# A new order of a software-pipelined period, with VectorE block transposes and three accumulating banks in the aggregation

## The chip, the cores and the metric

The kernel runs on one core of one Trainium2 chip. The metric is device time in microseconds for one execution. Five engines work side by side, each through its own queue in order: TensorE (PE; its weight loads are listed as PEld), VectorE (DVE), ScalarE (ACT), GpSimd (POOL) and SyncE (SP), which here only issues DMA transfers.

## The reference

There are 64 independent batches of 256 nodes with 512 features, all in 32-bit floats, and one 256x256 adjacency matrix. Two layers are applied to each batch, each as a residual step after a normalization and a ReLU:

```python
h = relu(layernorm(x))
x = x + gat(h, adj, W, a_src, a_dst)             # layer 0
h = relu(layernorm(x))
x = x + mha(h, adj, Wq, bq, Wk, bk, Wv, bv, Wo, bo)   # layer 1, 8 heads of 64

# gat:  Wh = h @ W; logits = leaky_relu(e_src[:, None] + e_dst[None, :], 0.2)
#       out = softmax(logits where adj else -inf) @ Wh
# mha:  q, k, v = h @ W.T + b; softmax(q k / 8 where adj) @ v; out @ Wo.T + bo
```

## The kernel before

**Tiling.** A batch is two row tiles of 128 nodes. Layer 0 first aggregates and then projects: `aggregate0` computes (attention weights) times h into `uT`, feature-major, and `transform0` multiplies `uT` by W and adds the rows to x. Layer 1 normalizes (`normalize1` writes `xn`), transposes to the feature-major `hT` (`transpose1`), projects (`project_qk`, `project_v`), attends (`attention`), divides by the row sums (`scale`) and projects back (`output`).

**Seven products.** Each big product of 2x2 blocks is computed with seven block products in place of eight. GpSimd forms four sums of the left blocks (`combine`: hs from hT, us from uT, as from aT, hq from h); the weight side is summed once. `chained` runs the seven in the order 0, 2, 1, 4, 3, 6, 5 and accumulates them in three PSUM banks called a, b and d: products 0, 1, 3, 5 go into bank a, product 2 into b, products 4 and 6 into d. A bank is read after each product, so the next product on the same bank must wait for that read. `assemble` does the reads: ScalarE copies after products 0, 1, 4, 5, VectorE adds after 2, 3, 6. In `transform0` and `output` VectorE makes all seven reads, each an add into x (line 768 before). The aggregation of layer 0 doesn't use `chained`: it uses `products`, with seven banks of its own and no accumulation, and `add_up`, which makes seven VectorE adds.

**The period.** One loop over i runs pieces of many batches at once. Each stage is a generator, and a list names which generator goes one step forward, and for which batch relative to i. The lists are written out by hand and nothing reorders them, so they fix the order in every engine's queue. The letters: K is `project_qk`, V `project_v`, W `transform0`, O `output` (seven products each); A is `attention` (a step for the scores and exponentials, four for masks and sums of two heads each, one for the values, the row sums and the transfers of the reciprocals); AS is `scale` (one step that multiplies, one that forms the sums); U0 and US are `aggregate0`; X1 is `transpose1`, N0 and N1 the normalizations, D0 the step that computes the two scores of the nodes and broadcasts one of them by DMA, E0 the edge weights, Q0 the quarters' sums, BO a bias.

```python
K, V, W, O = (project_qk, 0), (project_v, 0), (transform0, 1), (output, -2)
first_half = [
    (load, 3), O, D0, K, AS_OLD, O, K, O, K, O, K, E0, O, US, BO, A_OLD, K, E0, O, K, O, K,
]
second_half = [
    A_OLD, A, Q0, Q0, A, W, N0, W, W, V, N0, W, W, W, N1, W, N1, A, V, V, V, A, N0, N1, V, U0, AS,
    U0, X1, V, X1, V, X1,
]
```

**What crosses engines.** `attention` ends with the row sums `psm` on TensorE, reciprocals `rc` on VectorE, and twelve DMA issues of SyncE that broadcast them: four into `rb0` (for layer 0 of a later batch) and eight into `rb` (four for the first half of the heads, then four for the second). `scale` multiplies `aT[0]` and `aT[1]` by the halves of `rb` on VectorE; `output` needs `aT` so scaled, and from its third product on the GpSimd sums `as`. The tiles `hT`, `xn`, `uT`, `rb`, `rc`, `aT` and others have one buffer each (`h` has two, x six); the eight PSUM banks go round in the order in which they are asked for. A tile with one buffer is written for the next batch only when the last reader of the batch before has ended. For `hT` that reader is the last product of V.

Of the kernel before, what the change touches and what calls it, by code (L numbers as in the profile page):

```python
# [23 lines left out]
Q = 32  # L24
# [4 lines left out]
def kernel(  # L29
# [102 lines left out]
    def bounded():  # L132
# [34 lines left out]
            nc.gpsimd.tensor_tensor(s[:, 2], a(0, 0), a(1, 0), op=ALU.subtract)  # L167
            nc.gpsimd.tensor_tensor(s[:, 3], a(0, 1), s[:, 1], op=ALU.subtract)

        def products(a, s, name, product, read, order=range(7)):  # L170


            plan = (
                (a(0, 0), B11),
                (s[:, 1], T2),
                (a(0, 1), B21),
                (s[:, 2], T3),
                (s[:, 0], T1),
                (a(1, 1), T4N),
                (s[:, 3], B22),  # L180
            )
            for n in order:
                left, slot = plan[n]
                ps = bank([P, D], f"{name}_{n}")
                product(ps, left, slot)
                read(n, ps)
                yield

        CHAIN = ((0, "a"), (2, "b"), (1, "a"), (4, "d"), (3, "a"), (6, "d"), (5, "a"))

        def chained(a, s, name, product, read):
# [20 lines left out]
        def assemble(n, ps, dst, copy):  # L212
# [12 lines left out]
                nc.vector.tensor_add(dst(0, 1), dst(0, 1), ps)  # L225
            elif n == 5:
                copy(dst(1, 0), ps, 0)

        def add_up(n, ps, dst, s2):

            if n == 1:
                nc.vector.tensor_add(s2, dst(0, 0), ps)
            elif n == 2:
                nc.vector.tensor_add(dst(0, 0), dst(0, 0), ps)
            elif n == 3:
                nc.vector.tensor_add(dst(1, 0), s2, ps)
            elif n == 4:
                nc.vector.tensor_add(dst(1, 1), dst(1, 0), ps)
                nc.vector.tensor_add(dst(0, 1), s2, ps)
            elif n == 5:  # L240
                nc.vector.tensor_add(dst(1, 0), dst(1, 0), ps)
            elif n == 6:
                nc.vector.tensor_add(dst(0, 1), dst(0, 1), ps)

        def product_rows(wt, dst, left, slot, first):
            for c in range(2):
# [292 lines left out]
        def normalize0(g):  # L539

            xt = xts[g]
            h = big.tile([P, NT, D], F32, tag="h", name=f"h_{g}", bufs=2)
            es = small.tile([P, NT], F32, tag="es", name=f"es_{g}")
            ed = small.tile([P, NT], F32, tag="ed", name=f"ed_{g}")
            if g == 1:

                mv, rstd = norm_stats(xt, f"0_{g}", small)
                nmr = small.tile([P, NT], F32, tag="nmr", name=f"nmr0_{g}")
                nc.gpsimd.tensor_scalar(nmr, mv[:, :, 0], -1.0, 0.0, op0=ALU.mult, op1=ALU.add)
                nc.gpsimd.tensor_tensor(nmr, nmr, rstd, op=ALU.mult)  # L550
                yield
            else:
                stats = Stats(xt, h, f"0_{g}")
                for t in range(NT):
                    stats.mean(t)
                yield
                for t in range(NT):
                    stats.squares(t)
                nmr, rstd = stats.close()
                yield  # L560
            for t in range(NT):
                nc.scalar.activation(  # L562
                    h[:, t, :], xt[:, t, :], AF.Relu, bias=nmr[:, t : t + 1], scale=rstd[:, t : t + 1]
                )
            yield
            for t in range(NT):
                for dst, a in ((es, 0), (ed, 1)):
                    junk = work.tile([P, D], F32, tag="e2", name=f"junk_{g}_{t}")
                    nc.vector.scalar_tensor_tensor(  # L569
                        junk, (wa if g else pas)[a], 1.0, h[:, t, :], op0=ALU.mult, op1=ALU.mult,  # L570
                        accum_out=dst[:, t : t + 1],
                    )
            nodes[g] = h, es, ed
            if g >= PLAIN:

                row = work.tile([1, TOK], F32, tag="rc", name=f"es_row_{g}")
                for t in range(NT):
                    nc.sync.dma_start(row[:, t * P : (t + 1) * P], es[:, t : t + 1])
                es_b = work.tile([P, TOK], F32, tag="esum", name=f"es_b_{g}")
                spread(es_b, row)  # L580
                nodes[g] = h, es_b, ed
            yield
# [83 lines left out]
        def aggregate0(g):  # L666

            h, parts = nodes.pop(g)[0:2]
            em = edges[g][0]
            uT = big.tile([P, DC, TOK], F32, tag="uT", name=f"uT_{g}")  # L670
            if g >= PLAIN:
                left, s, right = parts
                s2 = work.tile([P, 4, P], F32, tag="s2", name=f"s2u_{g}")

                def product(dst, left, slot):
                    for e in range(2):
                        nc.tensor.matmul(
                            dst[:, e * P : (e + 1) * P], left[:, e * P : (e + 1) * P], right[slot],
                            start=True, stop=True,
                        )  # L680

                def dst(i, j):
                    return uT[:, 2 * i : 2 * i + 2, j * P : (j + 1) * P]

                def read(n, ps):
                    ps = ps[:, 0:HD].rearrange("p (e n) -> p e n", e=2)
                    if n == 0:
                        nc.scalar.copy(dst(0, 0), ps)
                    add_up(n, ps, dst, s2[:, 0:2, :])

                step_of = products(left, s, f"pu_{g}", product, read)
                for n in range(7):
                    next(step_of)
                    if n in (3, 6):
                        yield
                assert next(step_of, END) is END
            for dp in range(0, DC, 2) if g < PLAIN else ():
                pu = bank([P, 2, N], f"pu_{g}_{dp}")
                for d in range(2):
                    for m in range(NC):  # L700
                        nc.tensor.matmul(
                            pu[:, d, :],
                            h[:, m, (dp + d) * P : (dp + d + 1) * P],
                            em[:, m, :],
                            start=(m == 0),
                            stop=(m == NC - 1),
                        )
                nc.vector.tensor_mul(
                    uT[:, dp : dp + 2, :], pu, edges[g][1].unsqueeze(1).to_broadcast([P, 2, N])
                )  # L710
                yield

            def a(t, j):
                return uT[:, 2 * j : 2 * j + 2, t * P : (t + 1) * P]

            del edges[g]
            sums0[g] = a, four_sums("us", g)
            combine(a, sums0[g][1])
            yield
# [57 lines left out]
        def normalize1(g):  # L777
# [16 lines left out]
                xn = big.tile([P, NT, D], F32, tag="xn", name=f"xn_{g}")  # L794
            for t in range(NT):
                nc.scalar.activation(
                    xn[:, t, :], xt[:, t, :], AF.Identity,
                    bias=nmr[:, t : t + 1], scale=rstd[:, t : t + 1],
                )
            norms[g] = xn  # L800
# [4 lines left out]
        def transpose1(g):  # L805
# [5 lines left out]
            def a(t, j):  # L811
                return hT[:, 2 * j : 2 * j + 2, t * P : (t + 1) * P]

            for t in range(NT):
                pt = bank([P, DC, P], f"pt_{g}_{t}")
                for c in range(DC):
                    nc.tensor.transpose(pt[:, c, :], xn[:, t, c * P : (c + 1) * P], ident)
                nc.scalar.activation(hT[:, :, t * P : (t + 1) * P], pt, AF.Relu)  # L818
                yield
            lefts[g] = a, four_sums("hs", g)  # L820
            combine(a, lefts[g][1])
# [264 lines left out]
        def aside(n=1):  # L1086
            for _ in range(n):
                next(side, END)

        K, V, W, O = (project_qk, 0), (project_v, 0), (transform0, 1), (output, -2)  # L1090
        N0, D0, E0, U0 = (normalize0, 3), (normalize0, 2), (weights0, 2), (aggregate0, 2)
        Q0 = (quarters0, 2)
        US, N1, X1 = (aggregate0, 1), (normalize1, 1), (transpose1, 1)
        A, A_OLD, BO = (attention, 0), (attention, -1), (bias_rows, 0)
        AS, AS_OLD = (scale, -1), (scale, -2)
        first_half = [
            (load, 3), O, D0, K, AS_OLD, O, K, O, K, O, K, E0, O, US, BO, A_OLD, K, E0, O, K, O, K,
        ]
        second_half = [
            A_OLD, A, Q0, Q0, A, W, N0, W, W, V, N0, W, W, W, N1, W, N1, A, V, V, V, A, N0, N1, V, U0, AS,  # L1100
            U0, X1, V, X1, V, X1,
        ]

        OL = (output, -1)
        last = first_half + [
            A_OLD, A, V, V, A_OLD, A, A, V, V, V, V, V, AS, A, A, A, OL, OL, A, OL,
        ]
        end = [A_OLD, AS, O, OL, OL, OL, OL]


        S, E, L0, L1 = (normalize0, 0), (weights0, 0), (layer0, 0), (normalize1, 0)
# [16 lines left out]
        for i in range(G + 1):  # L1128
# [1 line left out]
                load_wo()  # L1130
            todo = first_half + second_half
            if i == 0:
                todo = first + [A, W, N0, E0] + second_half[7:17] + [(sums_of(wq_sb), 0)]
                todo += [V, V, V, N0, N1, V, U0, (sums_of(wk_sb), 0), U0, X1, V, A, X1, V, X1]
            elif i == 1:
                at = len(first_half) + 3
                todo[at:at] = [(sums_of(wo_sb, nc.gpsimd), 0)]
            elif i >= G - 1:
                todo = end if i == G else last
            for n, (stage, ahead) in enumerate(todo):  # L1140
                if i == 0 and n in (5, 10):
                    next(bias)
                if i == 0 and n == 12:
                    combine_w(wv_sb)
                if i == 1 and n in (4, 9):
                    step(attention, 0)
                if i == 1 and n == 13:
                    step(bias_rows, 0)
                step(stage, i + ahead)
                if i > 1 and n % 4 == 1:  # L1150
# [210 lines left out]
```

## Time and profile before

| | |
|---|---|
| median of 3 runs | 3077.15 us (3077.03 to 3077.54) |
| profiled execution | 3077.94 us, span 3076.2 us |
| busy: PE, PEld | 2915.8, 2532.1 us |
| busy: DVE, ACT, POOL | 1773.5, 1443.4, 1486.3 us |
| waits of PE for the GpSimd sums `as` | 115.3 us in 62 waits |
| transposes of `transpose1` on PE (line 817) | 512 instruction records, 77.0 us busy |

The span runs from the first to the last instruction of the program. A group in the profile names a source line, an engine and the tiles, with buffer numbers left out; `x4` counts instructions. One 32-bit matmul of the program appears as two matmul records. An idle time carries the name of what ended it.

### The profile page before, as it was taken

What the parts mean: (1) busy time and instruction counts of PE and PEld (TensorE: products, weight loads), DVE (VectorE), ACT (ScalarE), POOL (GpSimd) and SP (SyncE); (2) the same over time, 40 slices, a digit from 0 to 9 for tenths busy, and PEclk for the clock granted to TensorE, in tenths of its full rate; (3) what the DMA queues carried; (4) which work ended last, traced back from release to release, by engine and by line L of the source; (5) the groups of instructions that cost most, each with busy time, mean ns of one, the idle gap of its engine ahead of it and who ended that gap; (6) DMA issues with size and microseconds to landing.
All of it is one profiled execution on the core that took longest, in us unless ns stands there. A gap on an engine that the chain in (4) does not pass through costs nothing. (4 is left out here: it accounts for less than half of the span.)

```text
span 3076.2 us, 54206 instructions
## 1 busy us (share of the span) xinstructions
PE 2915.8 (95%) x20560; PEld 2532.1 (82%) x20560; DVE 1773.5 (58%) x3434; ACT 1443.4 (47%) x3729; POOL 1486.3 (48%) x2020
## 2 busy tenths in 40 slices
PE   9899999999999999999999999999999999999998
PEld 6788888888888888888888888888888888888886
DVE  6666565565555656556556555565555655655554
ACT  6445445454444544544545445454444454544532
POOL 2654554544545445455554454544545545445441
PEclk9999999999999999999999999999999999999999
DMA  3333233233332333323323333233332432333321
GB/s 124 29 40 47 34 41 41 40 40 38 38 47 33 41 39 36 47 34 41 46 36 40 37 38 47 33 41 38 37 47 34 42 47 34 40 37 39 40 39 29
DMA packets 144320, 127.15 MB, mean 41 GB/s; under 512 B 65204, under 2 KB 110132, under 8 KB 144054
## 3 DMA queue, kind: packets, MB, share of 16 engines
q1 hardware_dynamic: 143958, 123.61, 33.6%
q8 instruction: 165, 2.70, 0.3%
q14 instruction: 101, 0.83, 0.1%
q0 software_dynamic: 96, 0.01, 0.0%
HBM read 41.43 MB, written 33.55 MB: 24 GB/s over the span
## 5 line engine op out<-in xcount | busy, mean ns | idle before, releaser
L854 ACT ACTIVATE qk<-pqk_a,bias 128x128 f32<-128x128 f32 x756 | 215.5, 368 | 882.6 <-PE pqk_a L257 882.6
L768 DVE TENSOR_TENSOR x<-po_a,x 128x256 f32<-128x256 f32 x500 | 212.4, 425 | 376.4 <-PE po_a L247 372.4
L649 POOL TENSOR_TENSOR em<-em,rb 128x256 f32<-128x256 f32 x122 | 86.2, 727 | 625.1 <-DMA rb<-rc 625.1
L905 DVE TENSOR_TENSOR ex<-ex,maskT 128x512 f32<-128x512 f32 x512 | 330.0, 686 | 0.0
L900 ACT ACTIVATE ex<-psc 128x512 f32<-128x512 f32 x512 | 257.6, 627 | 96.2 <-PE psc L892 96.2
L569 DVE SCALAR_TENSOR_TENSOR junk<-wa,h 128x512 f32<-128x512 f32 x252 | 279.9, 1111 | 7.6 <-ACT h L562 0.9
L768 DVE TENSOR_TENSOR x<-po_d,x 128x256 f32<-128x256 f32 x250 | 105.9, 423 | 307.2 <-PE po_d L247 307.2
L247 PE MATMUL po_a<-wo_sb,as 128*128 128x256 f32 x496 | 149.1, 428 | 115.3 <-POOL as L166 115.3
L165 POOL TENSOR_TENSOR hs<-hT 128x256 f32<-128x256 f32 x64 | 47.3, 740 | 402.2 <-ACT hT L818 402.2
L892 PE MATMUL psc<-qk 64*128 64x256 f32 x2048 | 238.4, 383 | 0.0
L917 PE MATMUL pav<-ex,v 128*64 128x256 f32 x2048 | 235.5, 382 | 0.0
L952 DVE TENSOR_SCALAR rc<-psm 128x64 f32<-128x64 f32 x61 | 13.7, 225 | 373.7 <-PE psm L946 373.7
L608 POOL TENSOR_TENSOR em<-e,maskT 128x512 f32<-128x512 f32 x62 | 79.2, 1277 | 296.4 <-DVE e L605 286.6
L892 PEld LDWEIGHTS psc<-qk 64*128 64x128 f32 x2048 | 193.1, 187 | 26.3 <-ACT aT L925 0.8
L917 PEld LDWEIGHTS pav<-ex,v 128*64 128x64 f32 x2048 | 141.2, 137 | 73.1 <-issue 0.9
L247 PEld LDWEIGHTS po_a<-wo_sb,as 128*128 128x128 f32 x496 | 89.5, 200 | 134.8 <-POOL as L166 127.0
L907 DVE TENSOR_TENSOR sm<-ex 128x512 f32<-128x512 f32 x256 | 177.9, 695 | 8.9
L257 PEld LDWEIGHTS pqk_a<-hs,wq_sb 128*128 128x128 f32 x1008 | 168.9, 238 | 9.8
L818 ACT ACTIVATE hT<-pt 128x512 f32<-128x512 f32 x128 | 69.6, 595 | 215.1 <-PE pv_a L247 214.7
L257 PE MATMUL pqk_a<-hs,wq_sb 128*128 128x128 f32 x1008 | 170.3, 325 | 0.0
L995 POOL TENSOR_TENSOR x<-x,bo_b 128x512 f32<-128x512 f32 x128 | 161.5, 1283 | 0.0
L247 PE MATMUL pv_a<-wv_sb,hs 128*128 128x256 f32 x512 | 138.1, 392 | 24.4 <-ACT v L872 23.9
(231 smaller groups left out, 7460.4 us busy)
## 6 DMA issues: line engine op xcount, KB each, us to landing
x<-in_x_dram SPq DMA_DIRECT2D x64, 512.0 KB, 5.5
out_dram<-x SPq DMA_DIRECT2D x128, 256.0 KB, 2.0
rb<-rc SPq DMA_DIRECT2D x496, 64.0 KB, 5.1
es_b<-es_row SPq DMA_DIRECT2D x61, 128.0 KB, 6.4
rb<-rc SPq DMA_DIRECT2D x244, 32.0 KB, 3.8
es_row<-es SPq DMA_DIRECT2D x122, 0.5 KB, 2.0
wq_sb<-in_L_gnn_Wq_dram SPq DMA_DIRECT2D x4, 256.0 KB, 8.6
wk_sb<-in_L_gnn_Wk_dram SPq DMA_DIRECT2D x4, 256.0 KB, 6.7
```

The lines of the kernel that those rows point to most:

```text
L247: nc.tensor.matmul(dst[:, 0:HD], left[:, c, :], wt[:, slot, c, :], start=first and c == 0, stop=c == 1, skip_group_check=not first,)
L257: nc.tensor.matmul(dst[:, at : at + P], wt[:, slot, c, e * P : (e + 1) * P], left[:, c, :], start=first and at == 0 and c == 0, stop=c == ...
L569: nc.vector.scalar_tensor_tensor(junk, (wa if g else pas)[a], 1.0, h[:, t, :], op0=ALU.mult, op1=ALU.mult, accum_out=dst[:, t : t + 1],)
L649: nc.gpsimd.tensor_tensor(em[:, m, :], em[:, m, :], rb, op=ALU.mult)
L768: nc.vector.tensor_add(part, ps[:, 0:HD], part)
L854: nc.scalar.activation(to[:, c, :], ps[:, c, :], AF.Identity, bias=biases[j][:, c : c + 1])
L892: nc.tensor.matmul(psc[r][:, m, :], qk[rows, 2 + e % 2, m * P : (m + 1) * P], qk[rows, e % 2, :], start=True, stop=True,)
L900: nc.scalar.activation(ex[:, r, :, :], psc[r], AF.Exp, scale=SCALE)
L905: nc.vector.tensor_mul(ex[:, r, :, :], ex[:, r, :, :], maskT)
L907: nc.vector.tensor_add(sm, ex[:, :, 0, :], ex[:, :, 1, :])
L917: nc.tensor.matmul(pav[r * DH : (r + 1) * DH, i, :], v[j][:, m, at : at + DH], pair[i][:, r, m, :], start=(m == 0), stop=(m == NC - 1),)
L995: nc.gpsimd.tensor_tensor(part, part, bo_b, op=ALU.add)
```

## The change

There are four parts.

1. The lists of the period are new. O now works on the batch i-1 in place of i-2 and stands at the end of the period among V, X1 and U0; K stands alone at the start; both steps of AS lie in one period, before O; W's seven products stand together.
2. `aggregate0` uses `chained` and `assemble` (three banks; four ScalarE copies and three VectorE adds) in place of `products` and `add_up` (seven banks; one copy and seven adds).
3. `transpose1`, from batch 2 on, makes 16 VectorE transposes of 32x32 blocks (each instruction 32 partitions by 256 elements, SBUF to SBUF) in place of eight TensorE transposes and two ScalarE copies of 128x512 from PSUM. The ReLU moves into `normalize1`.
4. `normalize0` computes both halves of the first score before the second score.

```diff
-            for t in range(NT):
-                for dst, a in ((es, 0), (ed, 1)):
+            for dst, a in ((es, 0), (ed, 1)):
+                for t in range(NT):
...
-                def product(dst, left, slot):
+                def product(dst, left, slot, first):
                     for e in range(2):
                         nc.tensor.matmul(
                             dst[:, e * P : (e + 1) * P], left[:, e * P : (e + 1) * P], right[slot],
-                            start=True, stop=True,
+                            start=first and e == 0, stop=True, skip_group_check=True,
                         )
...
+                def copy(to, ps, j):
+                    nc.scalar.copy(to, ps)
+
                 def read(n, ps):
-                    ps = ps[:, 0:HD].rearrange("p (e n) -> p e n", e=2)
-                    if n == 0:
-                        nc.scalar.copy(dst(0, 0), ps)
-                    add_up(n, ps, dst, s2[:, 0:2, :])
...
+                    assemble(n, ps[:, 0:HD].rearrange("p (e n) -> p e n", e=2), dst, copy)
+
+                yield from chained(left, s, f"pu_{g}", product, read)
...
-                    xn[:, t, :], xt[:, t, :], AF.Identity,
+                    xn[:, t, :], xt[:, t, :], AF.Relu,
...
-            for t in range(NT):
+            for t in range(NT) if g < 2 else ():
                 pt = bank([P, DC, P], f"pt_{g}_{t}")
                 for c in range(DC):
                     nc.tensor.transpose(pt[:, c, :], xn[:, t, c * P : (c + 1) * P], ident)
-                nc.scalar.activation(hT[:, :, t * P : (t + 1) * P], pt, AF.Relu)
+                nc.scalar.copy(hT[:, :, t * P : (t + 1) * P], pt)
+                yield
+            rows = xn.rearrange("p t (c q f) -> p t c q f", q=4, f=Q)
+            cols_ = hT.rearrange("p c (t q n) -> p t c q n", t=NT, n=Q)
+            for i in range(4) if g >= 2 else ():
+                for j in range(4):
+                    nc.vector.transpose(
+                        cols_[j * Q : (j + 1) * Q, :, :, i, :], rows[i * Q : (i + 1) * Q, :, :, j, :]
+                    )
                 yield
...
-        K, V, W, O = (project_qk, 0), (project_v, 0), (transform0, 1), (output, -2)
+        K, V, W, O = (project_qk, 0), (project_v, 0), (transform0, 1), (output, -1)
...
-            (load, 3), O, D0, K, AS_OLD, O, K, O, K, O, K, E0, O, US, BO, A_OLD, K, E0, O, K, O, K,
+            (load, 3), K, D0, K, K, A_OLD, K, US, BO, K, K, E0, E0, K, A_OLD,
         ]
         second_half = [
-            A_OLD, A, Q0, Q0, A, W, N0, W, W, V, N0, W, W, W, N1, W, N1, A, V, V, V, A, N0, N1, V, U0, AS,
-            U0, X1, V, X1, V, X1,
+            A, A, Q0, N0, N0, Q0, W, W, W, W, W, W, N1, W, V, N1, AS, V, V, N0, V, N1, A, AS, A,
+            O, V, X1, O, X1, V, O, X1, V, O, X1, O, U0, U0, O, U0, U0, O, U0, U0, U0, X1,
         ]
```

In the queues this gives, from K to K. TensorE: K1 to K7, values, row sums, scores, W1 to W7, V1 to V4, O1, V5, O2, V6, O3, V7, O4, O5, U1, U2, O6, U3, U4, O7, U5, U6, U7. VectorE from the row sums on: reciprocals, mask of heads 0 and 1, seven adds of W, two multiplications by `rb`, add of V2, two more mask groups, add of O1, add of V5, four transposes, add of O2, four transposes, adds of V6 and O3, four transposes, add of O4, four transposes, add of O5, of U2, of O6, O7, U5, U6, then the four dot products of D0. SyncE: twelve reciprocal transfers, two stores, the load, the three transfers of the score.

## The prediction

> **What bounds the kernel now.** I read the engine totals first, then the table of waits, then the timeline of one period.
>
> ```profile
> PE 2915.8 (95%) x20560; PEld 2532.1 (82%) x20560; DVE 1773.5 (58%) x3434; ACT 1443.4 (47%) x3729; POOL 1486.3 (48%) x2020
> ```
>
> TensorE is busy nearly throughout. The table of waits shows what it waits for, and that VectorE and GpSimd wait a lot without holding it up:
>
> ```profile
> POOL em L649 <- DMA rb<-rc: 625.1, 61, 11.0
> DVE rc L952 <- PE psm L946: 373.7, 61, 7.4
> PE po_a L247 <- POOL as L166: 115.3, 62, 2.3
> ```
>
> The timeline of one period (columns: start, duration, engine, line, operation):
>
> ```profile
> 1522.50 0.23 DVE L952 TENSOR_SCALAR rc<-psm 128x64 f32<-128x64 f32 x1 [6.11 <-PE psm L946]
> 1523.40 10.27 SPq L497 DMA_DIRECT2D rb<-rc  x12
> ...
> 1541.00 1.29 DVE L1002 TENSOR_TENSOR aT<-aT,rb 128x512 f32<-128x512 f32 x2
> ...
> 1543.15 1.08 ACT L818 ACTIVATE hT<-pt 128x512 f32<-128x512 f32 x2 [3.41 <-PE pv_a L247]
> ```
>
> See two things. The twelve reciprocal transfers are issued over 10.27 us, and `aT<-aT,rb`, which needs them, stands 17.6 us after the first issue, with no idle time before it: that latency is covered. And the write of hT waits for V's last product, because hT has one buffer; here only ScalarE, which has time, stands behind that wait.
>
> Third, the TensorE clock:
>
> ```profile
> 1550.43 1.13 PE L247 MATMUL po_a<-wo_sb,as 128*128 128x256 f32 x4 [1.93 <-POOL as L166]
> ...
> 1596.65 1.13 PE L247 MATMUL po_a<-wo_sb,as 128*128 128x256 f32 x4 [1.92 <-POOL as L166]
> 1597.62 1.67 PE L257 MATMUL pqk_a<-hs,wq_sb 128*128 128x128 f32 x8
> 1599.08 1.91 PE L257 MATMUL pqk_a<-hs,wk_sb 128*128 128x128 f32 x8
> ```
>
> After the same gap of 1.9 us the products run slow for some 3.3 us in this period and normally (1.05 for eight) in the one before. By the starts of the scores, periods are 46.2 or 47.9 us long, most of them 47.9; from batch 1 (100.85) to batch 63 (3039.17) the mean of 62 is **47.39 us**.
>
> **What the Trainium skill says.** "VectorE: DVE Perf Modes", The three transpose paths: a VectorE transpose works on 32x32 blocks only, goes to SBUF, and takes 311 ns for 128x128 bf16. No row here shows one. The same page, Two Vector instructions with no wait between them: an instruction whose input or output starts in another group of 32 partitions than the last one's is held until everything before it has finished. All VectorE rows looked at here start at the same partition, so the trace doesn't show it; back to back, two adds of 0.42 start 0.34 apart. "TensorE: Matmul & The Clock Gate", Part 1: after an idle window of about 3.4 us the array runs at half clock, for a window. The trace agrees in form: a slow patch of about 3.3 us after a gap, costing 47.87 - 46.23 = 1.64 us; its gap was shorter, though, 1.9 us.
>
> **The change, part by part.**
>
> Removed from TensorE: eight transposes a period in two groups of 0.44 (1540.35 to 1540.78 and 1541.65 to 1542.09), 0.87 us in all, and the 1.9 us gap at `as`. ScalarE loses two copies (1.08) and gains three of about 0.36; it idles for more than half the span, so this costs nothing as long as it isn't on the path below, and it isn't. The three banks leave the aggregation's product count the same; VectorE loses four adds, 4 x 0.42 = 1.7 us. If nothing waited, TensorE would need its 46.23 less gaps (1.92, 0.38 and about 0.9 of small ones) less 0.87, some 42.5 us. So the question is what waits.
>
> Added to VectorE: 16 transposes of 256 elements. From the page's 311 ns for 128 elements, with 128 more at the rate of this trace's rows (128x256 add 418 ns, 128x512 add 686 ns, so 268 ns for 256), I estimate 0.44; the 128x256 row says 0.42. I take **0.43 each, 6.9 us**, held one by one. Bounds: 0.34 (overlapping like the adds) and 0.60 (268 ns more, if four-byte data took two passes).
>
> Now the new queues from one K to the next, time 0 at K1. TensorE: seven K at 1.78 end at 12.46; values from 12.56; row sums at 16.16 (3.60 later, as in 1517.65 to 1521.25); scores at 17.27; W1 at 20.93; seven W at 0.866 end at 26.99; V1 to V4 end at 30.46.
>
> *The reciprocals.* Before, the first issue comes 2.15 after the row sums start (1521.25, 1523.40). So the first issue is at 18.3. From it to the landing of the eighth transfer (first half of rb) the trace has 10.3 to 10.8, to the twelfth 14.4 to 15.2 us. The halves land at **28.9 and 32.8**. VectorE ends its last W add at 26.99 + 0.2 + 0.42 = 27.6, meets the multiplications, and idles 1.3 and then, after 0.69, another 3.2 us. It ends the second at 33.5. GpSimd's `as` follow while VectorE masks and are ready in time. The output was two batches behind and is now one; what hid the 14.5 us is gone.
>
> *What is queued behind.* TensorE makes O1 (30.5) and V5, then stands until 33.5 for O2 (gap 1.3). VectorE still has the add of V2 (0.42) and two mask groups (2 x 1.93) ahead of the add of O1, which ends at 38.2. O3 accumulates in O1's bank, so TensorE, done with V6 at 35.2, stands 3.0 us. O3 and V7 end at 39.95.
>
> *The transposes.* The first overwrites hT and waits for V7, 40.15 with 0.2 of latency; VectorE idles 1.5 us. Then come 16 transposes and the adds of O2, V6, O3, O4: 6.9 + 4 x 0.42 = 8.6, so hT is complete at 48.7. O5 shares a bank with O3, whose add comes after eight transposes and three adds, at 44.85; TensorE, done with O4 at 40.8, stands 4.0 us. O6 waits for O4's add (47.0), O7 for O5's (49.1), U7 for U5's (51.1). U7 ends at 51.6 and K1 follows. hs are not needed before K3.
>
> *Other queues.* SyncE's stores, load and score transfers come after the last adds; es lands some 6.4 us after its issue, about 10.8 into the next period, and ScalarE's exponentials, VectorE's maximum and GpSimd's products (0.7 + 2.0) reach the row sums' last part at about 15.5, needed at 17.0. Little margin, no stall. GpSimd's queue holds nothing else that is late. The swap in D0 only brings the score forward; I cost it nothing, since that margin covers it.
>
> *Clock.* Gaps of 3.0 and 4.0 us are both longer than the 1.9 that already brought a slow patch in most periods. The first patch would lie on O3 and V7 (up to 1.7), the second on O5 and U1, U2, with 0.9 of it left at U7. Bounds 0 and 2.6; I take half, 1.3.
>
> **Sum.** 51.6 + 1.3 = 52.9 us a period against 47.39: 5.5 x 62 = 342 us more. Start and end hold the same work. The profiled execution's own time, 3077.94, becomes 3420; the median of the runs, 3077.15, is 0.8 lower: **3419 us**.
>
> **Rivals.**
>
> *Milder: cheap transposes and an even clock.* At 0.34 the period is 51.6 - 1.4 = 50.2; with no patch 2.8 x 62 = 172 more, 3249 us. For: back-to-back adds do overlap. Against: every transpose changes its output's partition group. Between this and the main case lies a continuum.
>
> *Harsher: two passes for four bytes.* 0.60 gives 16 x 0.17 = 2.7 more: 55.6, or 509 more, 3586 us. Against: the page states no such doubling.
>
> *Faster: the transfers land early enough.* If the twelfth landed by 27.6, VectorE wouldn't stand: the multiplications end at 28.9, O1's add at 33.6, O3 starts when TensorE is free at 33.95, V7 is seen at 35.9 in place of 40.15, 4.25 earlier. With transposes at 0.34 and no slow patch the period is 45.9 and the kernel takes 1.5 x 62 = 92 us less, 2985. With cheap transposes it decides from a landing 2.8 us earlier than before's 14.5. For: all earlier transfers of the queue have landed. Against: the same was so before, and the shortest of the recorded landings is 14.4.
>
> That the change doesn't do what it says is excluded: the built queues contain the 16 transposes and the order above.
>
> **How the numbers follow.** Main case 0.70, milder 0.15, harsher 0.08, faster 0.06, no difference 0.01. A measurement can tell about 0.2%, 6 us. The range reaches from a period of 49.6 (3215) to one of 54.9 (3540): it takes in the milder case and the clock's bounds, and leaves out the faster and the harsher end. Faster 0.06, same 0.01, slower 0.93.
>
> **What would show it.** In the profile after: VectorE's `aT<-aT,rb` waiting for DMA rb, some 4 us a period; the transposes as a row of 992 near 0.43 us, the first of each sixteen waiting for TensorE's pv_a; po_a waiting for VectorE's x, with gaps of 3 and 4 us; TensorE's busy share under 88%, and slow patches after those gaps. I'd be wrong if rb landed before VectorE asked, if the transposes came far from 0.43, or if TensorE ran without gaps of over 2 us.

## The result, and the profile after

| | before | after |
|---|---|---|
| median | 3077.35 us (4 runs) | 3686.07 us (4 runs, 3682.89 to 3687.82) |
| ratio to before | | 1.1977 (95% interval 1.1956 to 1.1998) |
| span, mean granted clock of the profiled execution | 3076.2 us, 0.973 | 3684.2 us, 0.914 |
| mean period, batch 1 to 63, by the starts of the scores | 47.39 us | 57.17 us |

The changed kernel is slower by 609 us, and 62 x (57.17 - 47.39) = 606 of them lie in the repeated period. The forecast was 3419 us with a range up to 3540: the direction is right, the size is not. Two lines of the page of the kernel after show the shape, the engine totals and the granted TensorE clock in forty slices:

```profile
PE 3062.5 (83%) x20064; PEld 2589.5 (70%) x20064; DVE 2367.3 (64%) x4182; ACT 1450.1 (39%) x3788; POOL 1546.6 (42%) x2020
...
PEclk9989999989999898998999989989999898998999
```

TensorE's busy share fell from 95 to 83%. It issues fewer instructions than before, and yet is busy 147 us longer: the clock row now holds eights, where that of the kernel before has forty nines. The busy time of VectorE grew by 594 us, and only 432 of these are transposes. The groups of the pages say where the rest is (busy time and mean ns of one, then idle time ahead of it and what ended it). First the masks before:

```profile
L905 DVE TENSOR_TENSOR ex<-ex,maskT 128x512 f32<-128x512 f32 x512 | 330.0, 686 | 0.0
```

Then the kernel after:

```profile
L783 DVE STREAM_TRANSPOSE hT<-xn 32x256 f32<-32x256 f32 x992 | 432.4, 436 | 219.2 <-PE pv_a L212 204.3
L872 DVE TENSOR_TENSOR ex<-ex,maskT 128x512 f32<-128x512 f32 x512 | 544.9, 1103 | 0.0
```

The transposes take what was forecast (0.43). The masks, untouched by the change, take 1103 ns in place of 686. The table of waits of the kernel after (total, times, longest):

```profile
PE po_a L212 <- DVE x L727: 513.3, 125, 4.5
...
DVE aT L969 <- DMA rb<-rc: 249.6, 108, 3.8
DVE hT L783 <- PE pv_a L212: 204.3, 62, 3.7
```

These are the three waits of the forecast: VectorE for the reciprocals, VectorE's first transpose for V7, TensorE at O3 and O5 for VectorE's adds. From one period on TensorE (start, duration; O2, O3, V7, O4 and O5):

```profile
1838.48 1.10 PE L212 MATMUL po_b<-wo_sb,aT 128*128 128x256 f32 x4 [1.41 <-DVE aT L969]
...
1844.88 1.23 PE L212 MATMUL po_a<-wo_sb,as 128*128 128x256 f32 x4 [4.44 <-DVE x L727]
1845.90 1.91 PE L212 MATMUL pv_a<-wv_sb,hT 128*128 128x256 f32 x4
1847.61 1.79 PE L212 MATMUL po_d<-wo_sb,as 128*128 128x256 f32 x4
1852.88 2.04 PE L212 MATMUL po_a<-wo_sb,as 128*128 128x256 f32 x4 [3.48 <-DVE x L727]
```

After each of the two long gaps products run at 1.8 to 2.0 us in place of 1.03; after the first gap this begins one product later, on V7. What VectorE does ahead of O3, and GpSimd beside it, in the same period:

```profile
1837.64 0.69 DVE L969 TENSOR_TENSOR aT<-aT,rb 128x512 f32<-128x512 f32 x1 [3.29 <-DMA rb<-rc]
...
1838.58 2.24 DVE L872 TENSOR_TENSOR ex<-ex,maskT 128x512 f32<-128x512 f32 x2
1840.85 1.10 DVE L874 TENSOR_TENSOR sm<-ex 128x512 f32<-128x512 f32 x1
1841.87 1.81 DVE L872 TENSOR_TENSOR ex<-ex,maskT 128x512 f32<-128x512 f32 x2
...
1844.32 0.42 DVE L727 TENSOR_TENSOR x<-po_a,x 128x256 f32<-128x256 f32 x1
...
1847.95 1.78 DVE L783 STREAM_TRANSPOSE hT<-xn 32x256 f32<-32x256 f32 x4 [2.89 <-PE pv_a L212]
```

```profile
1838.41 0.72 POOL L165 TENSOR_TENSOR as<-aT,aT 128x256 f32<-128x256 f32 x1 [2.32 <-DVE aT L969]
1839.21 1.05 POOL L166 TENSOR_TENSOR as<-as,aT 128x256 f32<-128x256 f32 x1
1840.23 1.17 POOL L167 TENSOR_TENSOR as<-aT 128x256 f32<-128x256 f32 x1
1841.36 1.17 POOL L168 TENSOR_TENSOR as<-aT,as 128x256 f32<-128x256 f32 x1
```

The two mask groups end 5.8 us after they began; the forecast gave them 3.86. They stop being slow when GpSimd's last sum of `as` ends, and GpSimd's sums, 0.73 alone, are slow as well while VectorE works. The pair of masks that stands beside the bias adds early in the period is slower still (3.38 us), but behind it VectorE waits for TensorE (0.65 us in this period), so it costs the period nothing.

### The profile page after: what moved, and what is told of

It is laid out like the page before. It is cut to its first block, busy times and chain, and to the rows that moved or that the text cites. A ratio compares the mean times of both kernels' runs of the same rounds, so it can differ in the third digit from the quotient of the medians.

```text
span 3684.2 us, 54198 instructions
## 1 busy us (share of the span) xinstructions
PE 3062.5 (83%) x20064; PEld 2589.5 (70%) x20064; DVE 2367.3 (64%) x4182; ACT 1450.1 (39%) x3788; POOL 1546.6 (42%) x2020
## 5 line engine op out<-in xcount | busy, mean ns | idle before, releaser
L212 PE MATMUL po_a<-wo_sb,as 128*128 128x256 f32 x496 | 232.6, 619 | 512.9 <-DVE x L727 512.9
L783 DVE STREAM_TRANSPOSE hT<-xn 32x256 f32<-32x256 f32 x992 | 432.4, 436 | 219.2 <-PE pv_a L212 204.3
L872 DVE TENSOR_TENSOR ex<-ex,maskT 128x512 f32<-128x512 f32 x512 | 544.9, 1103 | 0.0
L212 PEld LDWEIGHTS po_a<-wo_sb,as 128*128 128x128 f32 x496 | 131.6, 292 | 581.4 <-issue 558.7
L650 ACT COPY uT<-pu_a 128x256 f32<-128x256 f32 x183 | 68.1, 372 | 746.2 <-PE pu_a L641 746.2
L839 ACT COPY v<-pv_a 128x256 f32<-128x256 f32 x192 | 68.8, 359 | 624.1 <-PE pv_a L212 624.1
L969 DVE TENSOR_TENSOR aT<-aT,rb 128x512 f32<-128x512 f32 x124 | 92.2, 743 | 274.1 <-DMA rb<-rc 249.6
L534 DVE SCALAR_TENSOR_TENSOR junk<-wa,h 128x512 f32<-128x512 f32 x252 | 247.9, 984 | 7.5 <-ACT h L527 0.9
L212 PE MATMUL po_d<-wo_sb,as 128*128 128x256 f32 x496 | 189.0, 522 | 0.2 <-DVE x L727 0.2
L962 POOL TENSOR_TENSOR x<-x,bo_b 128x512 f32<-128x512 f32 x128 | 188.9, 1495 | 0.0
```

What stands on the lines that cost most here:

```text
L212: nc.tensor.matmul(dst[:, 0:HD], left[:, c, :], wt[:, slot, c, :], start=first and c == 0, stop=c == 1, skip_group_check=not first,)
L534: nc.vector.scalar_tensor_tensor(junk, (wa if g else pas)[a], 1.0, h[:, t, :], op0=ALU.mult, op1=ALU.mult, accum_out=dst[:, t : t + 1],)
L783: nc.vector.transpose(cols_[j * Q : (j + 1) * Q, :, :, i, :], rows[i * Q : (i + 1) * Q, :, :, j, :])
L872: nc.vector.tensor_mul(ex[:, r, :, :], ex[:, r, :, :], maskT)
L962: nc.gpsimd.tensor_tensor(part, part, bo_b, op=ALU.add)
L969: nc.vector.tensor_mul(aT[j], aT[j], rb[:, 2 * j : 2 * j + 2, :])
```

## The experiments

Periods are the mean of 62, from batch 1 to batch 63. The first four kernels are the changed one with an edit. The theory at this point: of the 4.3 us by which the period exceeds the forecast, nearly 2 come from masks beside the sums, and over 1 from a clock that is lost after every gap, not after half of them.

### Masks ahead of the multiplication

```diff
-            A, A, Q0, N0, N0, Q0, W, W, W, W, W, W, N1, W, V, N1, AS, V, V, N0, V, N1, A, AS, A,
+            A, A, Q0, N0, N0, Q0, W, W, W, W, W, W, N1, W, V, N1, A, A, AS, V, V, N0, V, N1, AS,
```

> The two mask groups of heads 2 to 5 stand ahead of the two multiplications by rb on VectorE instead of behind them; nothing else moves. Theory (the chain from the row sums over the transfers, the multiplications and the masks to O1's add sets the period): the masks now fill the idle time before the second half of rb lands, O1's add comes about 5.5 us earlier, the 4.4 us gap of TensorE at O3 shrinks to under 1 us, and the period falls by 5.5 to 7 us from 57.2: 3250 to 3350 us. Rival (VectorE simply has too much work for the period, or TensorE's clock is what costs): the same work is done, so less than 1 us a period, above 3620 us.

Measured: 3517.93 us, ratio 1.1428 (1.1395 to 1.1462), period 54.47. This is half the gain expected. This kernel's TensorE timeline, at the two gaps of a period, says why:

```profile
1863.97 1.10 PE L212 MATMUL po_a<-wo_sb,aT 128*128 128x256 f32 x4 [2.51 <-DVE aT L969]
1864.90 1.68 PE L212 MATMUL pv_a<-wv_sb,hs 128*128 128x256 f32 x4
1866.38 1.91 PE L212 MATMUL po_b<-wo_sb,aT 128*128 128x256 f32 x4
...
1876.14 2.05 PE L212 MATMUL po_a<-wo_sb,as 128*128 128x256 f32 x4 [4.21 <-DVE x L727]
```

Now O1 itself waits for the multiplication, so O1 to O3 and V5 to V7 all follow it before the first transpose can start. The wait moved two products up, brought a slow patch of its own onto V5 and O2, and the chain behind V7 stayed whole. The expectation had counted the masks and had overlooked that O1 was running ahead of the second multiplication.

### The sums of `as` left out

The products of O that read `as` read a tile of zeros instead.

```diff
-            s = four_sums("as", g) if g < G - 2 else None
+            s = no_sums if g < G - 2 else None
...
-                combine(a, s)
```

> GpSimd's four sums as are left out: the products that use them read a tile of zeros that is written once, so this part of the output projection is not computed. Theory (the masks take 1.10 us instead of 0.69 because GpSimd works on SBUF beside them): the two mask groups after the multiplications fall from 5.7 to 3.9 us, the masks' mean from 1103 to about 850 ns (those beside other GpSimd work stay slow), and the period by about 1.8 us: 3560 to 3590 us. Rival (the masks are slow for another reason, ScalarE or the data's place): masks and time stay, 3680 us. If more than 3 us a period go, O3 also waited for the sums themselves.

Measured: 3519.50 us, ratio 1.1434 (1.1400 to 1.1467), period 54.52, clock 0.932. Its VectorE timeline, the two mask groups ahead of O1's add:

```profile
1808.27 1.29 DVE L874 TENSOR_TENSOR ex<-ex,maskT 128x512 f32<-128x512 f32 x2
...
1810.20 1.29 DVE L874 TENSOR_TENSOR ex<-ex,maskT 128x512 f32<-128x512 f32 x2
...
1812.13 0.42 DVE L729 TENSOR_TENSOR x<-po_a,x 128x256 f32<-128x256 f32 x1
```

The masks are back at 3.86 us for both groups, so it is the sums that slow them. The gain of 2.65 us is more than the 1.9 of the masks: the gap before O3 shrank from 4.4 to 2.5, and in 45 of 58 periods no slow patch followed it. The last section says which 13 it followed.

### The transposes back on TensorE

```diff
-            for t in range(NT) if g < 2 else ():
+            for t in range(NT):
...
-            for i in range(4) if g >= 2 else ():
+            for i in ():
...
-            O, V, X1, O, X1, V, O, X1, V, O, X1, O, U0, U0, O, U0, U0, O, U0, U0, U0, X1,
+            O, V, O, V, O, V, X1, O, X1, O, U0, U0, O, U0, U0, O, U0, U0, U0, X1,
```

> The new order with the transposes of batch 2 on back on TensorE and the copies on ScalarE, placed after V's last product. Theory: the 7 us of transposes leave VectorE's chain between V7 and O5, the gap of 3.5 us at O5 goes, 0.9 us of TensorE work comes back; the period falls by 4.5 to 6 us, 3310 to 3410 us, and O3's gap of 4.4 us stays. Rival (the transposes lie beside the waits for rb and cost nothing): within 1 us a period of 57.2, above 3620.

Measured: 3350.84 us, ratio 1.0886 (1.0854 to 1.0917), period 51.81, as the theory had it: the gap before O3 is still 4.4 us, the one before O5 is gone. New order and three banks together cost 273 us over before; the transposes bring the other 335.

### TensorE kept busy in the two gaps

```diff
-                yield from chained(a, s, f"po1_{g}", partial(product_rows, wo_sb), read)
-                return
+                steps_of = chained(a, s, f"po1_{g}", partial(product_rows, wo_sb), read)
+                for n in range(7):
+                    if 0 < g and n in (2, 4):
+                        busy(24)
+                    next(steps_of)
+                    yield
...
```

> Before O3 and before O5, where TensorE stands 4.4 and 3.5 us, it makes 24 transposes of the identity (2.6 us at full clock) into a bank that nothing reads. Theory (the slow products after a gap are a price of the gap): they vanish or shorten, granted clock above 0.96 from 0.914, and the period falls by 1.5 to 2.5 us: 3530 to 3595 us, faster with more work. Rival (the slow products come from elsewhere, such as operands still being written): no change or slower by what the filling overshoots, 3680 to 3750.

Measured: 3522.85 us, ratio 1.1444 (1.1411 to 1.1478), period 54.56, clock 0.996, a little faster than the theory's range. The dummy block and the product behind it, in this kernel's timeline:

```profile
1816.36 2.78 PE L309 MATMUL pbusy<-ident 128*128 128x128 f32 x24
1820.98 1.10 PE L212 MATMUL po_a<-wo_sb,as 128*128 128x256 f32 x4 [1.84 <-DVE x L727]
```

O3 still waits for the same add of VectorE, with 1.84 us of the gap left, but then it takes 1.10. Work was added to the bound engine and the kernel lost 163 us: 2.61 us a period is the price of the lost clock.

### Each part of the change by itself

The kernel before, with only the `as` sums moved:

```diff
-            (load, 3), O, D0, K, AS_OLD, O, K, O, K, O, K, E0, O, US, BO, A_OLD, K, E0, O, K, O, K,
+            (load, 3), O, D0, K, O, K, O, K, O, K, E0, O, US, BO, A_OLD, K, E0, O, K, O, K,
...
-            A_OLD, A, Q0, Q0, A, W, N0, W, W, V, N0, W, W, W, N1, W, N1, A, V, V, V, A, N0, N1, V, U0, AS,
+            A_OLD, A, Q0, Q0, A, W, N0, W, W, V, N0, W, W, W, N1, W, N1, A, V, V, V, A, N0, N1, V, U0, AS, AS,
```

> The kernel before with one step moved: the step that sums As for the next product (GpSimd's four sums of `as`) runs right after the multiplication by the reciprocals, instead of after the first K products of the next period. In the kernel before, the first aggregation product that reads `as` is held by these sums and a slow patch of TensorE follows. Theory (the order of the waits is what costs): the gap goes and with it the slow patch, the period falls from 47.4 to about 44.3 us, 62 x 3.1 = 191 us, so about 2885 us, bounds 2870 to 2960. Rival (the sums run beside VectorE's masks either way, and another operand, the sums hs or the third K product, takes over as the last thing waited for): 3000 to 3077 us.

Measured: 2870.99 us, ratio 0.9325 (0.9310 to 0.9341), period 44.06, clock 0.999. This version beats both kernels. Its page:

```profile
PE 2824.0 (98%) x20560; PEld 2455.8 (86%) x20560; DVE 1752.9 (61%) x3434; ACT 1452.9 (51%) x3729; POOL 1489.5 (52%) x2020
```

TensorE issues the same 20560 instructions as before; it is busy 92 us less because the slow patches are gone, and idle 115 us less because the wait is. A move of one step took away 3.33 us a period: 1.93 of gap; the patches that followed it in 45 of 57 periods, at 1.6 us, are 1.3 of the rest.

The kernel before, with the VectorE transposes alone (and the ReLU in `normalize1` that goes with them):

```diff
...
-            for t in range(NT):
+            for t in range(NT) if g < 2 else ():
...
+            for i in range(4) if g >= 2 else ():
+                for j in range(4):
+                    nc.vector.transpose(
+                        cols_[j * Q : (j + 1) * Q, :, :, i, :], rows[i * Q : (i + 1) * Q, :, :, j, :]
+                    )
+                if i % 2:
+                    yield
```

> The kernel before, in its old order and with its seven-bank aggregation, with VectorE's transposes in blocks of 32 as its only edit. Theory (the transposes cost their own 16 x 0.44 us and the wait of the first product of the next period behind them, plus a slow patch of TensorE): K1 waits for some 7 us of transposes after V7, less what the eviction and TensorE's transposes took before, so 4.5 to 5.5 us a period: 3350 to 3420 us. Rival (the transposes hide beside TensorE's products in any order, and only the new order puts them on the path): within 60 us of 3077.

Measured: 3479.68 us, ratio 1.1303 (1.1280 to 1.1325), period 53.89. K1 and the products after it in this kernel:

```profile
1803.13 2.04 PE L257 MATMUL pqk_a<-hT,wq_sb 128*128 128x128 f32 x8 [8.18 <-DVE hT L824]
1804.97 1.91 PE L257 MATMUL pqk_a<-hT,wk_sb 128*128 128x128 f32 x8
1806.68 1.43 PE L247 MATMUL po_b<-wo_sb,aT 128*128 128x256 f32 x4
```

The theory's wait is there and the size was missed by 60 us: the gap is 8.2 where 7 was taken, since an add stands between the two blocks of eight, and the patch after it costs 2.2. The new order, which spreads the transposes among the products of O, does better by the transposes than the old one (335 us against 401), but does not hide them.

The new order alone (three banks and VectorE transposes undone):

```diff
-                yield from chained(left, s, f"pu_{g}", product, read)
+                yield from products(left, s, f"pu_{g}", product, read)
...
-            O, V, X1, O, X1, V, O, X1, V, O, X1, O, U0, U0, O, U0, U0, O, U0, U0, U0, X1,
+            O, V, O, V, O, V, X1, O, X1, O, U0, U0, O, U0, U0, O, U0, U0, U0, X1,
```

> The new order alone: TensorE transposes and the aggregation with seven banks as before. Theory (the order alone costs what e3_pe_transposes showed, the banks cost nothing): within 40 us of 3351, so 3310 to 3390 us. Rival (the three-bank aggregation holds products by the reads of VectorE, and costs 1 us a period or more in the new order): under 3290 us.

Measured: 3314.90 us, ratio 1.0767 (1.0746 to 1.0789), period 51.23: the order alone costs 236 us, and the three banks in it 36 more. The time lies within the theory's 40 us of e3_pe_transposes.

The three banks alone, in the old order:

```diff
-                step_of = products(left, s, f"pu_{g}", product, read)
+                step_of = chained(left, s, f"pu_{g}", product, read)
```

> The kernel before with one edit: the quarter aggregation's seven products accumulate in three banks (aggregation with CHAIN and assemble) in place of seven banks; old order, transposes on TensorE. Theory (its products are moved among themselves and lie beside VectorE's free time): within 40 us of 3077. Rival (the three banks make each later product wait for VectorE's reads of the earlier one, 0.5 to 1 us a period, at each place): 3100 to 3150 us. In the new order the pair of e3_pe_transposes and e6_order_alone put the same edit at 36 us.

Measured: 3280.60 us, ratio 1.0655 (1.0637 to 1.0672), period 50.74. Both expectations were far too low. The aggregation in this kernel's TensorE timeline:

```profile
1845.51 0.61 PE L675 MATMUL pu_a<-em,h 128*128 128x128 f32 x4
...
1848.27 0.68 PE L675 MATMUL pu_a<-eq,hq 128*128 128x128 f32 x4 [1.70 <-ACT uT L684]
...
1852.15 1.06 PE L815 MATMUL pt<-ident,xn 128*128 128x128 f32 x4
```

From the first product to the transposes behind it are 6.6 us, against 3.2 with seven banks (in the timeline of b1_sums_early). The third product needs bank a, which ScalarE has yet to copy: 1.7 us of wait, and in 23 of 58 periods, this one among them, a slow patch behind it. The waits for that copy come to 104 of the 202 us; slow patches and shorter waits make up the rest. In the new order products of O stand between those of U and cover the wait.

### The reciprocals on TensorE

```diff
-                        spread(rb[r * DH : (r + 1) * DH, e, :], rc[at : at + 1, 0:N])
...
+            rb = [bank([P, N], f"prb_{g}_{e}") for e in range(DC)]
+            for e in range(DC):
+                rows = slice(e * Q, (e + 1) * Q)
+                nc.tensor.matmul(rb[e], pick[rows, :], rc[rows, 0:N], start=True, stop=True)
...
-            A, A, Q0, N0, N0, Q0, W, W, W, W, W, W, N1, W, V, N1, AS, V, V, N0, V, N1, A, AS, A,
+            A, A_OLD, A, AS, Q0, AS, N0, N0, Q0, W, W, W, W, W, W, N1, W, V, N1, V, V, N0, V, N1, A, A,
```

> The changed kernel with the reciprocals broadcast by TensorE into PSUM (as its last two batches do it) instead of by eight DMA transfers, and the multiplication right after the scores. Theory (in the new order the landing of rb sets when the masks and O1 to O7 can run, and all later waits hang on it): the multiplication ends about 7 us earlier than at 33.8 us into the period, the masks no longer stand between it and O1, and the period falls from 57.2 to about 50 us: about 3240 us, bounds 3150 to 3350. Rival (the chain after V7, 16 transposes and their readers, sets the period by itself, whatever rb does): 3560 to 3690 us.

Measured: 3311.24 us, ratio 1.0755 (1.0734 to 1.0777), period 51.15. The late landing of `rb`, with the place of the multiplication that goes with it, was worth 6.0 us a period. The gaps before O2 and O3 are gone, with the slow patch behind O3's, and the sums of `as` meet fewer of the masks (their mean is 953 ns in place of 1103); no run separates these shares. One gap of 4.2 us is left, before O5, behind the transposes.

### A second buffer for hT

```diff
-            hT = big.tile([P, DC, TOK], F32, tag="hT", name=f"hT_{g}")
+            hT = big.tile([P, DC, TOK], F32, tag="hT", name=f"hT_{g}", bufs=2)
...
```

In n1_two_hT on top of the reciprocals on TensorE, in n2_two_hT_alone on the changed kernel itself.

> n0_pe_broadcast with a second buffer for hT, so that the first transposes do not wait for V7's read of the old hT. Theory (the chain from V7 through 16 transposes sets what is left of the gap before O3): VectorE's wait of 1.92 us at the first transpose goes, the gap of 4.2 us before O3 shrinks to about 2.3, its slow patch shortens too: period 51.15 to about 48.7 us, 3311 to about 3160 us, bounds 3110 to 3200. Rival (O3's bank, read by VectorE between blocks of transposes, is what O3 waits for, and V7 is not on that path): 3290 to 3330 us.

> The changed kernel with a second buffer for hT as its only edit. Theory (after O1's add the transposes wait 2.9 us for V7, which is itself held behind O3's gap of 4.4 us): the transposes start 2.9 us earlier, K1 comes 2.5 to 3.5 us earlier, period 57.2 to about 54.3 us, 3686 to about 3507 us, bounds 3460 to 3560. Rival (O5 to O7 still come last, because VectorE's adds stand behind the blocks of transposes): over 3600 us.

Measured: n1_two_hT 3105.63 us, ratio to before 1.0089 (1.0069 to 1.0109), period 47.82; n2_two_hT_alone 3397.79 us, ratio 1.1038 (1.1016 to 1.1061), period 52.50. Both gain more than expected. The gap of 4.2 us that the expectation of n1_two_hT puts before O3 stands before O5; with the second buffer 2.2 of it are left. VectorE in n2_two_hT_alone, the last adds ahead of the first transposes:

```profile
1809.51 0.41 DVE L204 TENSOR_TENSOR v<-v,pv_a 128x256 f32<-128x256 f32 x1
1809.84 1.77 DVE L783 STREAM_TRANSPOSE hT<-xn 32x256 f32<-32x256 f32 x4
```

and TensorE at O3 and O5 of the same period:

```profile
1809.74 2.04 PE L212 MATMUL po_a<-wo_sb,as 128*128 128x256 f32 x4 [4.45 <-DVE x L727]
...
1814.78 1.10 PE L212 MATMUL po_a<-wo_sb,as 128*128 128x256 f32 x4
```

The transposes no longer wait 2.9 us for V7, and the gap before O5 is gone; with the gap went its slow patch, which the expectation had left out. The second buffer alone takes back 288 us of the 609. n1_two_hT, with both early reciprocals and two buffers, loses only 0.9% to before.

### Both causes of the miss at once

```diff
-            s = four_sums("as", g) if g < G - 2 else None
+            s = no_sums if g < G - 2 else None
...
+                    if 0 < g and n in (2, 4):
+                        busy(20 if n == 2 else 24)
```

> The changed kernel with both suspects of the missed forecast taken away together: GpSimd's sums of `as` are left out (O products read a tile of zeros), so the two mask groups ahead of O1's add run alone, and dummy transposes keep TensorE busy in the gaps before O3 (20) and before O5 (24), so that the clock stays. Theory (masks beside the sums +1.9 us, clock 2.7 us, independent of each other): e4_fill's full-clock period 54.56 less 1.9 is 52.6 us; 3523 less 62 x 1.9 is 3405 us, bounds 3380 to 3440. Rival (the two are one: without the sums the gaps are so short that the clock was never lost, as e2_no_as_sums' gain of 2.65 us would be in that case): within 20 us of 3520.

Measured: 3405.65 us (3399.59 to 3411.72), ratio 1.1064 (1.1041 to 1.1087), period 52.59, clock 0.996. The theory had 52.6 and 3405. Masks and clock are two separate terms.

## Why the prediction was wrong in size

In the terms of its sum, per period:

| term | forecast | measured | by |
|---|---|---|---|
| rest of the walk, at full clock | 51.6 | 52.6 | f1_fill_no_sums |
| masks beside the sums | 0 | 2.0 | e4_fill less f1_fill_no_sums, 54.56 - 52.59 |
| clock | 1.3 | 2.6 | after less e4_fill, 57.17 - 54.56 |
| period | 52.9 | 57.2 | |

The miss is 4.27 us a period, 265 us in 62, of the 267 by which the time was missed.

**The step that failed first** is the price of the mask groups: "two mask groups (2 x 1.93) ahead of the add of O1, which ends at 38.2". Their duration came from the row of before, where the same instructions stand beside GpSimd's tiny 128x2 steps or nothing. The prediction itself wrote that "GpSimd's `as` follow while VectorE masks", and treated it as cover, not as load. O1's add ended at 40.2. The trace of before had the sign of it: of GpSimd's 128x256 sums of `as`, 186 took 0.7 us and 61 took 1.2, and those of `hs` mostly 1.1 to 1.2, beside VectorE's dot products.

**The second step** is the clock: "Bounds 0 and 2.6; I take half, 1.3". Two gaps of 3.0 and 4.0 were forecast, both longer than the 1.9 that brought a patch most times, so half had no ground. By the clock's steps in the last section, a gap of 4.0 brings a patch nearly wherever it falls and one of 3.0 at about seven of ten positions; an estimate from that is 0.7 x 1.7 + 0.9 = 2.1, not 1.3. Counted over the periods of the kernel after, a slow patch followed all 116 gaps of 3.4 to 4.5 us, and cost TensorE about 2.1 us each; 2.6 of the 4.1 reached the period, because O4's share falls into the wait for O5. The upper bound was the right value, and the range ended below what the first step's miss and the rest of the walk added to it.

**The rest of the walk** came out 1.0 too short. The second multiplication ended at 33.8 (forecast 33.5), the sixteen transposes took 7.1 (6.9), hence 0.5; the other 0.5 was not traced to a step. Two slips in the prediction's sums carry no weight: the 42.5 without waits comes to 42.2 by its own figures, and the milder rival's 2.8 x 62 to 174.

**What held.** In the period shown, K1 is at 1804.55. The first transfer is issued at 18.3 (forecast 18.3); VectorE stands at both halves of `rb`; the gap at O2 is 1.4 (1.3); O3 waits for O1's add, the first transpose for V7, O5 for O3's add behind eight transposes. A transpose takes 436 ns (430), four in 1.78: consecutive ones do not overlap, as the Trainium skill's "VectorE: DVE Perf Modes", Two Vector instructions with no wait between them, says for changing partition groups, while two adds of 0.42 start 0.34 apart. The trace of n2_two_hT_alone shows that it is not the transpose as such: in all 62 periods the first of the sixteen, which reads and writes from the first partition on as the add ahead of it does, starts 0.08 us before that add has ended, and the other fifteen, whose input or output starts in another group, all start at least 0.013 us after the end of what stands ahead of them, transpose or add. So the milder and the harsher rival fell on their price of a transpose, though the time came out beyond the harsher one (3586), by other terms. The faster rival needed `rb` by 27.6; it came at 33.

**What was taken as free.** The three banks cost 36 us in the new order and 202 in the old. The sentence that they "leave the aggregation's product count the same" did not ask which product waits for which read. The prediction got away with it because the new order covers the wait.

The change gave away three covers at once: O two batches behind covered the reciprocals' transfers, ScalarE covered the wait of hT for V7, seven banks covered the reads. What it removed from TensorE was 0.87 us of transposes and one gap of 1.9. b1_sums_early shows that the gap was to be had without the rest.

## What to carry to other kernels

When a step moves in an order, price it with the neighbours of its new place: look in the trace for the same instruction beside the same other engine, and take that duration. Before spending a rewrite on a gap, follow its releaser and try to move that one step: here the sums of `as`, run one place earlier, gave 206 us. And if TensorE is the bound, count each gap of some 1.7 us and more at its length plus the slow patch that can follow it. Filling such a gap can pay even with work that nobody needs.

## What the runs showed of the hardware

VectorE's elementwise instructions with two SBUF inputs and GpSimd's slow each other. A 128x512 mask takes 0.68 us alone or beside GpSimd steps of 128x2, 1.10 to 1.21 beside GpSimd's 128x256 sums, and 1.70 beside its 128x512 bias adds; the sums go from 0.73 to 1.17. With the sums left out the masks beside them return to 0.68. An add with one input in PSUM is not slowed: `x<-po_a,x` takes 0.42 alone (272 in the kernel after) and 0.42 beside the 128x256 sums (76).

Which gap brings a slow patch is not a matter of its length alone. All 58 gaps of 8.2 us in b3_transposes_alone and all of 3.4 to 4.5 us in the kernel after, in e3_pe_transposes and in n0_pe_broadcast did. Of shorter gaps, all 58 of 2.5 us in e1_masks_first did, and 13 of 58 as long in e2_no_as_sums; 38 of 58 of 2.2 to 2.7 us in n1_two_hT; 45 of 57 near 1.9 us in the kernel before; 23 of 58 near 1.7 us in b2_banks_alone; and none of 115 of 1.6 to 1.9 us behind the dummy products of e4_fill.

What decides besides the length is where the gap falls, and the traces hold it. In all 14 of them the granted clock is either 1.0 or 0.5, and the instants at which it changes lie whole multiples of 3.413 us apart from the first change to the last, whatever the kernel does. Cut into these steps, two neighbouring periods of e2_no_as_sums, each with its gap of 2.47 us before O3, look like this (start and end, length, busy time of TensorE, granted clock, DMA):

```profile
1808.65:1812.07 3.42, 1.49 (x7) 1.00 0.00 0
1812.07:1815.48 3.41, 2.86 (x12) 1.00 0.01 2
...
1863.26:1866.68 3.42, 1.40 (x7) 1.00 0.00 0
1866.68:1870.09 3.41, 2.96 (x7) 0.50 0.00 0
```

In the first period 1.92 us of the gap lie in one step, and the clock stays; in the second 2.02 do, and the next step runs at half clock. So it is in all 58: the 13 gaps with at least 2.02 us in one step brought a patch, the 45 with at most 2.00 did not. Over the repeated periods of all 14 traces, each of the 656 steps at full clock that left TensorE idle, by its records, for more than 2.02 us was followed by a step at half clock, and none of the 10768 with less than 1.75 us idle was; of the 238 between, some were. Half clock lasts until a step with less than 0.62 us idle.

This fits the dummy products of e4_fill, which leave at most 1.85 us of a gap in one step, and e1_masks_first, whose period of 54.6 us is 16 steps, so that its gaps met the steps at nearly the same place each time. The prediction cites an idle window of about 3.4 us; the length of the step agrees, but a step idle for some 2 us is enough here. After a short gap the patch can begin 1 us into the products, as on V5 in e1_masks_first, because it begins with the next step. What decides within the narrow band between 1.75 and 2.02 us stays open.
